# Three edits to the scan stages of a four-layer network: one transfer for B and C, an earlier first map, norm products set apart

## The chip, the cores and the metric

The kernel runs on one core of a Trainium2 chip. The metric is device time in microseconds (us) of one execution, as the median of several runs; lower is better. A profile of one execution was taken besides. Engines are named as in the profile: PE (TensorE, matmuls; PEld its weight loads), DVE (VectorE), ACT (ScalarE), POOL (GpSimd) and SP (SyncE, which here only issues transfers). "Chunk", "step" and "tile" are explained below.

## The reference, cut to what matters

The input is 8 images of 64 channels by 64 x 64 pixels, all in float32, and passes through four layers. Layer 0 is a spectral layer that the change leaves alone. Layers 1, 2 and 3 are built around a selective scan over a sequence with 16 states per channel. Layer 1 scans each image in four ways, layer 2 once, and layer 3 in two stages (along one image axis and then the other), each forward and backward. The core of all of them is this, with layer 3's norm ahead of it:

```python
def rms_norm(x, w):
    return x * lax.rsqrt(jnp.mean(x * x, axis=-1, keepdims=True) + EPS) * w
...
xc = silu(causal_dwconv(xc, cw, cb))          # the "first map" and its convolution
dbl = xc @ xpw.T                              # dt's low-rank part, B and C
dt = jax.nn.softplus(dbl[..., :r] @ dtw.T + dtb)
Bm = dbl[..., r:r + n]
Cm = dbl[..., r + n:r + 2 * n]
A = -jnp.exp(Alog)
...
h = h * dA + (dt_t * x_t)[:, :, None] * B_t[:, None, :]     # dA = exp(dt * A), for each position
y = jnp.einsum('bdn,bn->bd', h, C_t)
...
y = (y + Dp * xc) * silu(z)
```

## The kernel before, in words

**Steps and tiles.** Every scan stage runs through one function, `stream` (L404). Its work is a list of steps. A step is 128 channels by 1024 positions (in layer 3: 256 channels by 512, put side by side). For each of the 16 states n, a step has one tile, 128 x 1024; the text counts tiles by n, and calls the time of one tile a slot. A tile takes these operations:

- SP broadcasts row n of B and of C from HBM to 128 partitions, as `bc`, or as `b` and `c` in layer 1 (L1220, L1602, L1985).
- POOL multiplies B with du = dt * u into `hb` (L465), three tiles ahead in layers 2 and 3, two in layer 1.
- ACT computes `dA` = exp(A * dt) into one of two PSUM buffers (L472), two tiles ahead.
- DVE scans (L481), in place in `dA`, or, for "shared" tiles, into `h`. Shared are tiles 1, 4, 7, 10, 13 of a step; in layer 3's backward steps 2, 6, 10, 14.
- The product with C (L495) is made by DVE, or by POOL for shared tiles.
- PE adds the product to the PSUM tile `acc` with a matmul by the identity (L287), two slots after the scan; a new step begins with a "skip" matmul of u. In layers 1 and 2, ACT copies each scan's last column into `carry` (L1230, L1611) for the step that follows in the same sequence.

When tile 2 of the next step has been scanned, DVE takes the finished `acc` of the last one (the drain: `img` at L1247, `z` at L1620 in layer 2 and L1994 in layer 3).

**What runs beside the tiles.** The order of instructions on each engine is written by hand: `stream` walks the slots, and in each it also lets other generators go on by one piece, up to their next `yield`. The first is `prepare` of the next step, which starts at slot `start`. In layer 2 it loads `x0` with two transfers on SP (L1560), makes the first map `px` on PE (L1567), applies a silu into `u` on ACT (L1570), multiplies u by the weights that give dt's part, B and C (`dbl`, copied out of PSUM by ACT at L1575), sends B and C to HBM in `bc` (L1578; in layer 1 L1203 and L1206), makes `dt` (a softplus, L396), `du` on POOL and the gate `z`. The second is the queue `behind`: in layer 1 the norms and the feed-forward part of other images, in layer 3 `begin` (L1852). A piece that says `CALM` waits for a slot in which neither this tile nor the next is shared; pieces that need the one PSUM buffer `mm` wait for each other; `yield False` lets a slot pass.

**Layer 3's norm.** A chunk is half an image, 8 steps (four groups, each forward and backward). While it is scanned, `begin` prepares the next one: it loads `raw`, squares it, takes means on PE (`ms`), gathers them in `rs`, a square root on ACT (L1879), a reciprocal on DVE (L1881), then sends `rs` to HBM (L1884) and back as a broadcast, `inv` (L1888, two transfers), and POOL multiplies `raw` by `inv` into `xn` in four products of 128 x 560 (L1896), in four slots that follow each other.

**Pools.** Tiles of a name come from a pool with a fixed number of buffers (`dA` 2 in PSUM, `hb` 4, `hc` 4, `bc` 8 in layers 2 and 3); semaphores are put in by the program builder where a buffer is used again. Which buffer a tile gets is also the builder's choice.

Of the kernel before, what the change touches and what calls it, by code (L numbers as in the profile page):

```python
# [10 lines left out]
F32 = mybir.dt.float32  # L11
# [10 lines left out]
NS = 16  # L22
T = 1024
# [226 lines left out]
class Net:  # L250
# [589 lines left out]
    def layer1(self, src, dst):  # L840
        nc, tc, d = self.nc, self.tc, self.d
        mid = self.hbm["x1a"]
        with ExitStack() as ctx:
# [317 lines left out]
            behind = deque()  # L1161
# [21 lines left out]
            class Step:  # L1183
# [12 lines left out]
                def prepare(self):  # L1196
                    k = self.k
                    u = self.u = view(images[self.b]["u"], k, self.c)
                    pd = pp.tile([128, T], F32, name="mm")[:68]
                    net.mm(pd, xp[:, k, :], u)  # L1200
                    yield True
                    dbl = p1.tile([68, T], F32, name="dbl")
                    nc.scalar.copy(dbl, pd)  # L1203
                    self.bc = hp.tile([NS, 2, T], F32, name="bc")
                    for m in range(2):
                        nc.scalar.dma_start(self.bc[:, m, :], dbl[4 + m * NS : 4 + m * NS + NS])  # L1206
                    pt = pp.tile([128, T], F32, name="mm")
                    for r in range(2):
                        at, o = slice(r * C, r * C + 4), slice(r * 512, r * 512 + 512)
                        nc.tensor.matmul(pt[:, o], dtw[at, k, :], dbl[at, o], start=True, stop=True)  # L1210
                    yield True
                    yield CALM
                    dt = self.dt = p2.tile([128, T], F32, name="dt")
                    net.softplus_act(dt, pt, dtb[:, k : k + 1])
                    yield False
                    du = self.du = p2.tile([128, T], F32, name="du")
                    nc.gpsimd.tensor_tensor(like(du, u), like(dt, u), u, ALU.mult)

                def load(self, n, m, t):
                    nc.sync.dma_start(t, self.bc[n : n + 1, m, :].to_broadcast([128, T]))  # L1220

                def first(self, n):
                    if n == 0:
# [274 lines left out]
    def l2_scan(self, hx, hy):  # L1498
        nc, tc, d = self.nc, self.tc, self.d
        with ExitStack() as ctx:  # L1500
# [34 lines left out]
            carries = {}  # L1535

            class Step:
                bc_shape, start, early, late = [128, 2, T], 1, 0, False
                shared = (1, 4, 7, 10, 13)
                rev = False  # L1540
                shaped = staticmethod(lambda t: t)
                spread = staticmethod(lambda t, m: t[:, m, :])
                lanes = [(slice(None), A)]
# [4 lines left out]
                def ready(self):  # L1548
                    pass

                def prepare(self):
                    b, c = self.b, self.c

                    x0 = self.x0 = p2.tile([128, T + 4], F32, name="x0", bufs=3)
                    for r in range(2):
                        lo = c * T - 3 - r
                        if c == 0:
                            nc.gpsimd.memset(x0[r * C : r * C + C, : 3 + r], 0.0)
                        skip_ = max(0, -lo)
                        nc.sync.dma_start(x0[r * C : r * C + C, skip_ : T + 3 + r], hx[b, :, lo + skip_ : c * T + T])  # L1560
                    yield False
                    yield
                    px = pp.tile([128, T], F32, name="mm")
                    for o in (0, 512):
                        for m in range(2):
                            f = o + 3 - 2 * m
                            nc.tensor.matmul(px[:, o : o + 512], taps[:, m, :], x0[:, f : f + 512], start=m == 0, stop=m == 1)  # L1567
                    yield CALM
                    u = self.u = p2.tile([128, T], F32, name="u")
                    nc.scalar.activation(u, px, AF.Silu, bias=cb)  # L1570
                    pd = pp.tile([128, T], F32, name="mm")[:68]
                    net.mm(pd, xp, u)
                    yield True
                    dbl = p1.tile([68, T], F32, name="dbl")
                    nc.scalar.copy(dbl, pd)  # L1575
                    self.bc = hp.tile([NS, 2, T], F32, name="bc")
                    for m in range(2):
                        nc.scalar.dma_start(self.bc[:, m, :], dbl[4 + m * NS : 4 + m * NS + NS])  # L1578
                    pt = pp.tile([128, T], F32, name="mm")
                    for r in range(2):  # L1580
                        at, o = slice(r * C, r * C + 4), slice(r * 512, r * 512 + 512)
                        nc.tensor.matmul(pt[:, o], dtw[at], dbl[at, o], start=True, stop=True)
                    yield CALM
                    dt = self.dt = p2.tile([128, T], F32, name="dt")
                    net.softplus_act(dt, pt, dtb)
                    yield
                    du = self.du = p2.tile([128, T], F32, name="du")
                    nc.gpsimd.tensor_tensor(du, dt, u, ALU.mult)
                    pz = pp.tile([128, T], F32, name="mm")
                    for r in range(2):  # L1590
                        at, f = slice(r * C, r * C + C), 3 + r + r * 512
                        nc.tensor.matmul(
                            pz[:, r * 512 : r * 512 + 512], w_in[at, 128:], x0[at, f : f + 512], start=True, stop=True
                        )
                    yield True
                    yield CALM
                    z = self.z = p2.tile([128, T], F32, name="z", bufs=3)
                    nc.scalar.activation(z, pz, AF.Silu)

                def load(self, n, t):  # L1600
                    row = self.bc[n : n + 1].rearrange("o m t -> o (m t)")
                    nc.sync.dma_start(t.rearrange("p m t -> p (m t)"), row.to_broadcast([128, 2 * T]))  # L1602

                def first(self, n):
                    if n == 0:
# [19 lines left out]
            net = self  # L1625
            with tc.manual_schedule():
                steps = [Step(b, c) for b in range(NB) for c in range(4)]
                self.stream(pools, (6, 3, 6), steps, deque())

    def leaky(self, out, ps):  # L1630
# [157 lines left out]
    def l3_stage(self, s, src, dst):  # L1788
# [6 lines left out]
        with ExitStack() as ctx:  # L1795
# [56 lines left out]
            def begin(c):  # L1852

                b, part = divmod(c, 2)
                q, rows = b // 2, slice((b % 2) * C, (b % 2) * C + C)
                x = raw[c % 2]
                hold = chunks[c] = {"x": x}
                from_ = src[q, rows, part * 4 * W : (part + 1) * 4 * W].rearrange("p (s t) -> p s t", t=HW)
                for r in range(2):
                    nc.sync.dma_start(x[r * C : r * C + C, :, ends[r]], from_)  # L1860
                yield False
                yield False
                rs = p1.tile([128, 16], F32, name="rs")
                for j in range(2):
                    yield CALM_FREE
                    sq = p1.tile([C, T], F32, name="sq")
                    o = sq.rearrange("p (s t) -> p s t", t=HW)
                    nc.scalar.activation(o, x[:C, j * 2 * H : (j + 1) * 2 * H, ends[0]], AF.Square)
                    yield
                    ps = pp.tile([128, T], F32, name="mm")  # L1870
                    self.mm(ps[:1, :], mean, sq)
                    yield CALM
                    ms = p1.tile([1, T], F32, name="ms")
                    nc.scalar.copy(ms, ps[:1, :])
                    yield False
                    nc.sync.dma_start(rs[j * 64 : j * 64 + 64], ms.rearrange("o (p e) -> o p e", e=16))
                yield False
                yield CALM_FREE
                nc.scalar.activation(rs, rs, AF.Sqrt, bias=self.eps5)  # L1879
                yield False  # L1880
                nc.vector.reciprocal(rs, rs)  # L1881
                yield False
                row = hp.tile([1, 4 * W], F32, name="rs")
                nc.sync.dma_start(row.rearrange("o (p e) -> (o p) e", e=16), rs)  # L1884
                yield False
                yield False
                for r in range(2):
                    nc.sync.dma_start(  # L1888
                        inv[r * C : r * C + C, :, ends[r]], row.rearrange("o (s t) -> o s t", t=HW).to_broadcast([C, 4 * H, HW])
                    )  # L1890
                yield False
                yield False
                hold["xn"] = p2.tile([128, 4 * H, HW + 6], F32, name="xn")
                for g in range(4):
                    at = slice(g * H, g * H + H)
                    nc.gpsimd.tensor_tensor(hold["xn"][:, at], x[:, at], inv[:, at], ALU.mult)  # L1896
                    yield False

            behind = deque()
            begun = {}  # L1900
# [162 lines left out]
```

## Time and profile before

| | |
|---|---|
| Median of 3 runs | 25114.63 us (25111.57 to 25133.84) |
| The profiled execution's own time | 25139.42 us |
| Its span | 25137.3 us |
| Busy: DVE, POOL, PE, ACT | 90%, 88%, 85%, 59% of the span |
| Layer 1's scans | about 1245 to 8590 us |
| Layer 2's scans | about 9060 to 10820 us |
| Layer 3's two stages | about 11710 to 25137 us |

Busy time is the time in which an engine executes; the rest is idle, and the profile tells for each instruction how long its engine stood idle before it and what ended that. Two or three engines that are each almost fully busy feed one another through a few buffers, so a wait of one of them can be made good later, or not, depending on how far ahead it was.

### The profile page before, as it was taken

Reading aid. Unit: us, or ns where it says so; the run is one execution under the profiler, and the core shown is the slowest. Engines: PE = TensorE matmul, PEld = TensorE weight load, DVE = VectorE, ACT = ScalarE, POOL = GpSimd, SP = SyncE. Lnnn points to the kernel's source line nnn. Section 1 sums busy time; section 2 is a strip of 40 time slices with the busy share of each in tenths; the row PEclk is TensorE's granted clock in tenths of the full one; section 3 lists DMA queues with packets and bytes.
Section 4 is the critical chain, followed back from the end, with each engine's and each line's share of the span. In section 5 each row is a group of like instructions: output and inputs, shape, how many; then the busy total and the mean of one; then the engine's idle time right before and its main releaser. Section 6 shows DMA issues by size and latency. Waiting matters only on the chain. (4 is left out here: it accounts for less than half of the span.)

```text
span 25137.3 us, 193414 instructions
## 1 busy us (share of the span) xinstructions
PE 21345.1 (85%) x53146; PEld 8321.9 (33%) x53146; DVE 22518.6 (90%) x13020; ACT 14745.8 (59%) x18563; POOL 21997.8 (88%) x10775
## 2 busy tenths in 40 slices
PE   8777888888888888888888888888888888888888
PEld 6522333333333323322333333333333333333333
DVE  5389999989989679978999999999989999999999
ACT  4355555555555455524666666666656666666666
POOL 0099999999989669977999999999989999999999
PEclk9888999999999999999999999999989999999999
DMA  2289898898889658833555545555445554555554
GB/s 64 86 309 320 309 320 313 307 314 314 311 312 314 225 218 323 326 111 87 168 170 168 170 168 171 169 170 168 167 155 171 166 171 165 173 166 172 166 171 158
DMA packets 1772400, 5282.72 MB, mean 210 GB/s; under 512 B 536352, under 2 KB 542564, under 8 KB 1703472
## 3 DMA queue, kind: packets, MB, share of 16 engines
q1 hardware_dynamic: 1744176, 5207.00, 61.0%
q10 hardware_dynamic: 27136, 63.34, 0.8%
q8 instruction: 423, 6.93, 0.1%
q14 instruction: 665, 5.45, 0.1%
HBM read 5112.85 MB, written 156.11 MB: 210 GB/s over the span
## 5 line engine op out<-in xcount | busy, mean ns | idle before, releaser
L465 POOL TENSOR_TENSOR hb<-du,bc 128x1024 f32<-128x1024 f32 x4608 | 10751.5, 2357 | 481.9 <-DVE h L481 330.0
L287 PE MATMUL acc<-hc,ident 128*128 128x512 f32 x18816 | 8899.3, 615 | 93.9 <-DVE img L1247 66.6
L472 ACT ACTIVATE dA<-dt,w_A 128x512 f32<-128x512 f32 x8192 | 5661.7, 691 | 4106.0 <-DVE hc L495 3120.0
L481 DVE TENSOR_TENSOR_SCAN dA<-dA,hb 128x1024 f32<-128x1024 f32 x3384 | 7725.9, 2283 | 285.1 <-ACT dA L472 121.9
L287 PE MATMUL acc<-h,ident 128*128 128x512 f32 x7808 | 4545.1, 712 | 2344.5 <-POOL h L495 2344.1
L287 PEld LDWEIGHTS acc<-hc,ident 128*128 128x128 f32 x18816 | 3695.7, 200 | 5305.9 <-issue 4670.3
L465 POOL TENSOR_TENSOR hb<-du,b 128x1024 f32<-128x1024 f32 x2048 | 4832.7, 2387 | 526.3 <-DVE h L481 279.3
L495 DVE TENSOR_TENSOR hc<-dA,bc 128x1024 f32<-128x1024 f32 x3296 | 4035.6, 1224 | 255.0 <-issue 4.0
L472 ACT ACTIVATE dA<-dt,w_l_A 128x1024 f32<-128x1024 f32 x2560 | 2856.3, 1117 | 1186.5 <-DVE hc L495 757.4
L481 DVE TENSOR_TENSOR_SCAN dA<-dA,carry,hb 128x1024 f32<-128x1024 f32 x1320 | 3094.7, 2344 | 171.2 <-ACT carry L1230 112.3
L287 PEld LDWEIGHTS acc<-h,ident 128*128 128x128 f32 x7808 | 1546.3, 215 | 5004.0 <-POOL h L495 3136.3
L481 DVE TENSOR_TENSOR_SCAN h<-dA,hb 128x1024 f32<-128x1024 f32 x1352 | 3082.5, 2280 | 46.3 <-ACT dA L472 41.4
L495 POOL TENSOR_TENSOR h<-h,bc 128x1024 f32<-128x1024 f32 x1312 | 3090.2, 2355 | 14.5 <-DVE h L481 14.5
L495 DVE TENSOR_TENSOR hc<-dA,c 128x1024 f32<-128x1024 f32 x1408 | 1723.5, 1224 | 114.9 <-DMA c<-bc 4.4
L495 POOL TENSOR_TENSOR h<-h,c 128x1024 f32<-128x1024 f32 x640 | 1516.3, 2369 | 7.4 <-ACT carry L1230 6.5
L481 DVE TENSOR_TENSOR_SCAN h<-dA,carry,hb 128x1024 f32<-128x1024 f32 x600 | 1404.8, 2341 | 80.7 <-ACT dA L472 75.5
L472 ACT ACT_TABLE_LOAD x1122 | 1439.5, 1283 | 21.0 <-ACT tmp L1016 1.2
L1230 ACT COPY carry<-dA 128x1 f32<-128x1 f32 x1056 | 167.9, 159 | 1725.7 <-DVE hc L495 1666.0
L1930 PE MATMUL mm<-xn,taps 128*128 128x512 f32 x2048 | 938.8, 600 | 33.6 <-POOL xn L1896 31.4
L702 POOL MEMSET xf<- 128x24 f32 x33 | 4.3, 142 | 855.8 <-PE ps L723 699.8
L1945 PE MATMUL mm<-u,w_xp 128*36 128x512 f32 x1024 | 519.6, 632 | 146.4 <-ACT u L1942 141.8
L1965 POOL TENSOR_TENSOR du<-dt,u 128x1024 f32<-128x1024 f32 x256 | 602.0, 2352 | 18.9 <-ACT dt L396 18.9
(310 smaller groups left out, 18559.8 us busy)
## 6 DMA issues: line engine op xcount, KB each, us to landing
bc<-bc SPq DMA_DIRECT2D x4096, 512.0 KB
b<-bc SPq DMA_DIRECT2D x2048, 512.0 KB
c<-bc SPq DMA_DIRECT2D x2048, 512.0 KB
bc<-bc SPq DMA_DIRECT2D x512, 1024.0 KB
tmp<-rs SPq DMA_DIRECT2D x93, 512.0 KB
raw<-x SPq DMA_DIRECT2D x64, 512.0 KB
inv<-rs SPq DMA_DIRECT2D x64, 512.0 KB
tmp<-x SPq DMA_DIRECT2D x192, 128.0 KB
```

The source lines that it names most:

```text
L287: self.nc.tensor.matmul(o, lhsT, r, start=start, stop=stop)
L465: nc.gpsimd.tensor_tensor(s.shaped(hb[i]), s.shaped(s.du), B.pop(i), ALU.mult)
L472: nc.scalar.activation(dA[i][:, cut], s.dt[:, cut], AF.Exp, scale=A[:, n : n + 1])
L481: nc.vector.tensor_tensor_scan(h[:, way], dA[i][:, way], hb.pop(i)[:, way], s.first(n), ALU.mult, ALU.add)
L495: engine.tensor_tensor(s.shaped(o), s.shaped(h), CC.pop(i), ALU.mult)
L702: nc.gpsimd.memset(x[:, :, HW:], 0.0)
L1230: nc.scalar.copy(self.carry[:, n : n + 1], h[:, last : last + 1])
L1930: nc.tensor.matmul(tokens(px[:, j * W : j * W + W]), taps[k][:, m, j * 128 : j * 128 + 128], xn[:, :, f : f + HW], start=m == 0, stop=m == 1,)
L1945: nc.tensor.matmul(pd, xp[:, k, j, :], u[:, j * W : j * W + W], start=j == 0, stop=j == 1)
L1965: nc.gpsimd.tensor_tensor(du, dt, u, ALU.mult)
```

## The change

1. In layers 1 and 2, `bc` in HBM becomes 32 rows (16 of B, then 16 of C) in place of 16 rows of pairs, and ACT sends it with one transfer of 32 rows in place of two of 16. Layer 2's broadcast of B and C, still one transfer of 1 MB for each tile, then reads two rows that lie apart; layer 1's reads are as before.
2. In layer 2, a step's `x0` is loaded at the end of `prepare` of the step before (`fetch`, with a fourth buffer), and `prepare` begins with the first map. It starts at slot 2 in place of 1, but has lost two pieces, so that the map stands one slot earlier, ahead of the drain.
3. In layer 3, one more slot passes between the square root and the reciprocal, and nine slots pass after each of the first three products by `inv` in place of one.

```diff
 # layer 1
-                    self.bc = hp.tile([NS, 2, T], F32, name="bc")
-                    for m in range(2):
-                        nc.scalar.dma_start(self.bc[:, m, :], dbl[4 + m * NS : 4 + m * NS + NS])
+                    self.bc = hp.tile([2 * NS, T], F32, name="bc")
+                    nc.scalar.dma_start(self.bc, dbl[4 : 4 + 2 * NS])
...
-                    nc.sync.dma_start(t, self.bc[n : n + 1, m, :].to_broadcast([128, T]))
+                    nc.sync.dma_start(t, self.bc[m * NS + n : m * NS + n + 1, :].to_broadcast([128, T]))
 # layer 2 (its bc is written as in layer 1)
-                bc_shape, start, early, late = [128, 2, T], 1, 0, False
+                bc_shape, start, early, late = [128, 2, T], 2, 0, False
+                behind = None
...
-                def prepare(self):
+                def fetch(self):
                     b, c = self.b, self.c
-                    x0 = self.x0 = p2.tile([128, T + 4], F32, name="x0", bufs=3)
+                    x0 = self.x0 = p2.tile([128, T + 4], F32, name="x0", bufs=4)
...
                         nc.sync.dma_start(x0[r * C : r * C + C, skip_ : T + 3 + r], hx[b, :, lo + skip_ : c * T + T])
-                    yield False
-                    yield
+                def prepare(self):
+                    x0 = self.x0
                     px = pp.tile([128, T], F32, name="mm")
...
                     nc.scalar.activation(z, pz, AF.Silu)
+                    if self.behind:
+                        self.behind.fetch()
                 def load(self, n, t):
-                    row = self.bc[n : n + 1].rearrange("o m t -> o (m t)")
-                    nc.sync.dma_start(t.rearrange("p m t -> p (m t)"), row.to_broadcast([128, 2 * T]))
+                    rows = self.bc.rearrange("(m n) t -> n m t", m=2)[n : n + 1]
+                    nc.sync.dma_start(t, rows.to_broadcast([128, 2, T]))
...
+                for step, other in zip(steps, steps[1:]):
+                    step.behind = other
+                steps[0].fetch()
 # layer 3, begin
                 nc.scalar.activation(rs, rs, AF.Sqrt, bias=self.eps5)
                 yield False
+                yield False
                 nc.vector.reciprocal(rs, rs)
...
                     nc.gpsimd.tensor_tensor(hold["xn"][:, at], x[:, at], inv[:, at], ALU.mult)
-                    yield False
+                    for _ in range(9 if g < 3 else 1):
+                        yield False
```

More of the change, by code (lines that the diff above doesn't have):

```diff
@@ L1575, in prepare @@
                     nc.scalar.copy(dbl, pd)
-                    self.bc = hp.tile([NS, 2, T], F32, name="bc")
-                    for m in range(2):
-                        nc.scalar.dma_start(self.bc[:, m, :], dbl[4 + m * NS : 4 + m * NS + NS])
+                    self.bc = hp.tile([2 * NS, T], F32, name="bc")
+                    nc.scalar.dma_start(self.bc, dbl[4 : 4 + 2 * NS])
                     pt = pp.tile([128, T], F32, name="mm")
```

## The prediction

> **What bounds the kernel now.** I read the page first (busy time, then the costliest groups), then the busy times by stage, then each scan's waits, then the order in time around those waits.
>
> ```profile
> PE 21345.1 (85%) x53146; PEld 8321.9 (33%) x53146; DVE 22518.6 (90%) x13020; ACT 14745.8 (59%) x18563; POOL 21997.8 (88%) x10775
> ...
> L465 POOL TENSOR_TENSOR hb<-du,bc 128x1024 f32<-128x1024 f32 x4608 | 10751.5, 2357 | 481.9 <-DVE h L481 330.0
> ```
>
> DVE and POOL both carry the span. By stage (columns: length, then busy time and count of PE, PEld, DVE, ACT and POOL, clock, DMA share, GB/s) these are layer 1's scans, layer 2's, and layer 3's second half:
>
> ```profile
> 1245.00:8590.00 7345.00, 6196.51 (x13857) 2333.71 (x13858) 6658.71 (x3717) 3900.18 (x4865) 6736.96 (x2960) 0.92 0.89 313
> 9060.00:10820.00 1760.00, 1423.96 (x3054) 542.66 (x3056) 1618.54 (x896) 1026.12 (x1241) 1632.98 (x718) 0.90 0.84 322
> 18460.00:25137.00 6677.00, 5744.65 (x11990) 2180.78 (x11989) 6445.34 (x3661) 4434.87 (x5768) 6456.22 (x2935) 0.94 0.52 168
> ```
>
> Neither engine can be shortened here, only DVE's waits can go: 686 us in layer 1, 142 in layer 2, some 520 in layer 3. The view of waits names them; the first three lines are layer 3's, the next three layer 2's.
>
> ```profile
> DVE z L1994 <- PE acc L287: 157.7, 41, 5.6
> DVE rs L1881 <- ACT rs L1879: 49.6, 31, 16.9
> DVE dA L481 <- POOL hb L465: 8.1, 10, 1.8
> ...
> DVE h L481 <- ACT dA L472: 59.7, 28, 4.6
> DVE dA L481 <- ACT carry L1611: 26.5, 20, 2.3
> ...
> ACT L1570 <- PE mm L1567: 87.6, 30, 3.4
> ```
>
> **Part 1, one transfer (layers 1 and 2).** It removes 160 DMA issues from ACT (two took 0.78 us in layer 1, 0.90 in layer 2). An issue in itself is worth little, since ACT then mostly waits for DVE. The order of instructions with their semaphores shows more. In layer 1 the dA that follows the pair of issues (tile 5) often waits not for tile 3's readers but for tile 4's scan, since the pool gave it tile 4's PSUM buffer. One such step in the order in time (ACT, then DVE):
>
> ```profile
> 1842.72 1.12 ACT L472 ACTIVATE dA<-dt,w_l_A 128x1024 f32<-128x1024 f32 x1 [2.10 <-DVE h L481]
> ...
> 1843.94 2.36 DVE L481 TENSOR_TENSOR_SCAN dA<-dA,carry,hb 128x1024 f32<-128x1024 f32 x1 [1.25 <-ACT carry L1230]
> ```
>
> ACT was free 2.10 us earlier; DVE loses the 1.25 us in which dA is made. Counted in the two orders, 88 of layer 1's steps have this wait in the old kernel and 43 in the new one; layer 2 keeps its 24. So 45 x 1.25 = 56 us; POOL idles 1 to 2 us in most such steps, so it follows nearly all the way. I take **-54** (bounds -30, if POOL binds, and -56). Other steps of layer 1 keep their waits.
>
> The same edit makes layer 2's loads read two rows of 4 KB where they read one of 8 KB: 256 packets for 128. In the trace's DMA packets a packet of 8192 bytes takes 334 ns on average in layer 2; of 4096 bytes, 185 in layer 1's loads. A load on 16 engines is then 16 x 185 = 2.96 us for 8 x 334 = 2.67, plus 0.22 a tile of other packets (111 us of 16 engines over 512 tiles): 3.18 against the 3.27 us a tile that I forecast for layer 2. POOL waited for loads 6 times, 5.9 us in all, and loads run six tiles ahead, so I cost it at 0; without that cover it is the third rival.
>
> **Part 2, layer 2's first map.** Its px matmuls move on PE from behind the drain, the skip and tile 1's gather to ahead of them; PE stood 4.3 us there waiting for the drain (9515.54), so they cost PE nothing. ACT's order does not change. ACT's silu waited for px 30 times, 2.9 us each; now it starts 2.65 us earlier (9523.52 for 9526.17), and the scan of tile 7, which lost 1.9 to 2.5 us to it, finds its dA. Next late is dA of tile 8: in 24 steps it shares tile 7's buffer and can't start before that scan ends, so 24 x 1.25 = 30 us stay. Layer 2's DVE waits, 104.9 us in the view (the above and 11.5, 7.2), less 5 at the start and these 30, leave 70. POOL, 51.0 us busy a step, has room below the 52 that DVE then needs. The x0 transfers (two issues of 0.59 us on SP) go out a step earlier, into a fourth buffer: 0. I take **-62** (-20 to -70; the low end if the buffers between POOL and DVE turn half of it into other waits).
>
> **Part 3, layer 3.** 30 of the 32 chunks run beside scans. Their step (drain to drain) lasts 57.1 us on average, the same step without products 50.64. The excess, 6.5: z 4.74, reciprocal 1.09, hb 0.26, the reciprocal itself 0.2, small ones. Here are two products, then the drain:
>
> ```profile
> 12325.25 1.37 POOL L1896 TENSOR_TENSOR xn<-raw,inv 128x560 f32<-128x560 f32 x1 [1.93 <-DMA inv<-rs]
> ...
> 12328.88 1.37 POOL L1896 TENSOR_TENSOR xn<-raw,inv 128x560 f32<-128x560 f32 x1
> ...
> 12354.56 1.22 DVE L1994 TENSOR_TENSOR z<-acc,z 128x1024 f32<-128x1024 f32 x1 [4.37 <-PE acc L287]
> ```
>
> *The reciprocal* moves behind one more scan and product, 3.5 us, so its 1.09 us wait goes: 33 us. But ACT's chain there (silu, sqrt, three table loads) ends dA at 12304.76, and a DVE no longer held up asks for it at 12304.5: 0.3 comes back. Net -24. The transfers behind it (SP: one row, two inv) move one tile with it, and so does the first product; POOL waited for inv 0.4 us a chunk, and I leave that.
>
> *The products*: 4 x 1.37 = 5.5 us of POOL in four tiles delay the h products, hence PE's last gather and the drain. In the new order they stand before h(10), after h(13), after h(6) of the next pair and after h(14). POOL regains 0.64 + 0.69 + 1.16 = 2.5 us a pair in its waits for DVE, so the first and the third each reach h(14) as a lag of 1.37. Two lines of PE tell what that does, without products and with:
>
> ```profile
> 12135.72 1.98 PE L287 MATMUL acc<-h,ident 128*128 128x512 f32 x4 [2.73 <-POOL h L495]
> ...
> 12764.47 3.78 PE L287 MATMUL acc<-h,ident 128*128 128x512 f32 x4 [4.37 <-POOL h L495]
> ```
>
> PE's wait becomes 2.73 + 1.37 = 4.10. All 14 waits of 4.0 to 4.5 us in layer 3 (the shortest 4.19) were followed by slow matmuls (1.06 us and more a record); at 3.0 to 3.5 most stayed at 0.6. Slow, acc is ready 6.15 us after h(14)'s end (12764.4 to 12770.6); fast, 3.54. DVE arrives 6.42 after it when POOL is on time. So the drain waits 1.37 - 0.27 = 1.1 us, twice a chunk. The second and fourth stand behind their step's last h; the drain they can delay has 1.6 to 3.3 us to spare against a lag of 1.0: 0.1. Hence 2.3 for 4.74 + 0.26: -81. Together **-105** (bounds -50, if lags add up, and -177, if PE stays fast).
>
> [...] The 14 of 14 rows speak for slow each time.
>
> **Sum.** 54 + 62 + 105 = 221. Against the profiled execution (25139.4, span 25137.3) that is 24,918; it lies 24.8 above the runs' median, so I give **24,895**.
>
> **Rivals.**
> - *The products vanish altogether*: if at 4.10 us PE stays fast, 3.54 + 1.37 is below 6.42 and no drain waits: 69 us more, 24,825. For it: the wait of 3.91 began fast. Against it: all from 4.19 up are slow.
> - *Waits change places*: POOL, at 51 us a step beside DVE's 52, becomes the bound in layers 1 and 2, and lags add up in layer 3: 30 + 20 + 50 = 100, so 25,015. For it: POOL shows only 0.1 us idle in one of layer 1's steps. Against it: layer 3's ordinary steps run without any DVE wait at the same load.
> - *Layer 2's loads become the bound* (slower): if 4 KB packets there take what layer 2's other 4 KB packets take, 245 ns, a load is 3.92 + 0.22 = 4.14 us a tile for 3.44 now: 512 x 0.70 = +358 in place of -62, so 25,115 + 358 - 54 - 105 = 25,314. It decides from 191 ns a packet on (16 x 191 + 220 = 3.27), and the whole is slower than before from 220 or so. Against it: layer 1 at 185 and a DMA share of 0.89 hardly waits. That margin is thin.
> - *The edit does not do what it says*: not here; the order shows each move.
>
> **Chances.** Forecast 0.62, first rival 0.17, second 0.12, third 0.05, something unseen 0.04. The range reaches from the first rival to past the second, widened by the bounds: 24,810 to 25,040. About 0.2%, 50 us, is what a measurement of this kernel can tell from no change: faster 0.90, same 0.05, slower 0.05.
>
> **What would show it.** Layer 2 (9060 to 10820) some 60 us shorter, with ACT's wait for px gone and tile 8's 1.25 left in 24 steps; layer 1 with 45 fewer 1.25s; in layer 3 no rs wait, z waits halved and near 1.1 each, at twice as many places. Wrong: long POOL waits for bc in layer 2, or z waits of 4 us.

## The result, and the profile after

| | before | after |
|---|---|---|
| Median | 25118.15 us (25111.57 to 25133.84, 4 runs) | 24936.65 us (24932.17 to 24940.46, 4 runs) |
| Profiled execution, its span | 25139.42, 25137.3 | 24935.87, 24934.1 |
| Layer 1, first scan to last | 7336.1 | 7293.2 (-43.0) |
| Layer 2 | 1746.6 | 1678.1 (-68.5) |
| Layer 3, two stages | 6659.5 + 6668.4 | 6622.3 + 6612.7 (-93.0) |

The ratio is 0.9925, interval 0.9913 to 0.9936: 182 us faster by the medians, 203 by the two profiled spans. Between the stages nothing moved by more than 2.7 us. Stage lengths, here and below, are from the start of the stage's first scan to the end of its last.

The page of the changed kernel, its busy times and the group that answers to the one shown of before:

```profile
PE 21183.9 (85%) x53146; PEld 8266.9 (33%) x53146; DVE 22534.6 (90%) x13020; ACT 14735.8 (59%) x18563; POOL 22026.2 (88%) x10775
...
L465 POOL TENSOR_TENSOR hb<-du,bc 128x1024 f32<-128x1024 f32 x4608 | 10740.3, 2356 | 294.6 <-DVE h L481 186.5
```

DVE's and POOL's work is what it was (22534.6 for 22518.6, 22026.2 for 21997.8); only idle time went. POOL's idle time ahead of these products fell from 481.9 to 294.6 us. By stage (the columns as before: length, busy times with counts, clock, DMA share, GB/s), layer 1, layer 2, and layer 3's second half:

```profile
1245.00:8547.00 7302.00, 6171.31 (x13860) 2327.64 (x13860) 6656.41 (x3717) 3899.89 (x4865) 6778.05 (x2960) 0.92 0.90 315
9021.00:10713.00 1692.00, 1403.56 (x3051) 524.64 (x3050) 1615.75 (x896) 1021.13 (x1239) 1631.30 (x718) 0.93 0.96 334
18312.00:24934.10 6622.10, 5680.84 (x11991) 2163.27 (x11989) 6449.07 (x3661) 4432.22 (x5768) 6448.86 (x2934) 0.95 0.51 169
```

Layer 2's DMA share rose from 0.84 to 0.96 with the shorter steps and the two rows a load. Its waits of DVE (time, times, longest), where before had 59.7, 26.5 and 11.5 us in three lines of dA and carry:

```profile
DVE dA L481 <- ACT carry L1613: 36.8, 30, 3.5
DVE dA L481 <- POOL hb L465: 25.3, 1, 25.3
DVE z L1622 <- PE acc L287: 2.1, 1, 2.1
DVE dA L481 <- ACT dA L472: 1.9, 3, 1.3
```

The 25.3 is the stage's first tile. What ACT's silu waited for is gone, as its line in time shows: the table load and the silu follow each other with no idle time in brackets.

```profile
9466.43 1.28 ACT L1571 ACT_TABLE_LOAD   x1
9467.73 1.11 ACT L1571 ACTIVATE u<-mm,w_l_cb 128x1024 f32<-128x1024 f32 x1
```

Layer 3's waits of DVE, first scan to last:

```profile
DVE dA L481 <- ACT dA L472: 76.4, 34, 33.8
DVE z L2002 <- PE acc L287: 51.2, 68, 3.9
DVE h L481 <- ACT dA L472: 42.1, 53, 0.8
DVE rs L1887 <- ACT rs L1884: 16.8, 1, 16.8
```

The drain (z) waits 51.2 us where it waited 154.9; the reciprocal's wait is down to one at the start of a stage; and a wait that before hardly had (5.2 us) has come, h for dA, 42.1 us. POOL got one too. The view of POOL's waits in layer 3's scans, before and then after:

```profile
POOL xn L1896 <- DMA inv<-rs: 50.8, 12, 39.7
```

```profile
POOL xn L1902 <- DMA inv<-rs: 93.5, 31, 39.2
```

Without the one long wait at a stage's start, that is 11.1 us in 11 chunks before, and 54.3 in 30 after: nearly every chunk, 1.8 us each.

### The profile page after: what moved, and what is told of

The parts are those of the page before. It is cut to its first block, busy times and chain, and to the rows that moved or that the text cites. A ratio compares the mean times of both kernels' runs of the same rounds, so it can differ in the third digit from the quotient of the medians.

```text
span 24934.1 us, 193361 instructions
## 1 busy us (share of the span) xinstructions
PE 21183.9 (85%) x53146; PEld 8266.9 (33%) x53146; DVE 22534.6 (90%) x13020; ACT 14735.8 (59%) x18563; POOL 22026.2 (88%) x10775
## 5 line engine op out<-in xcount | busy, mean ns | idle before, releaser
L465 POOL TENSOR_TENSOR hb<-du,bc 128x1024 f32<-128x1024 f32 x4608 | 10740.3, 2356 | 294.6 <-DVE h L481 186.5
L495 DVE TENSOR_TENSOR hc<-dA,c 128x1024 f32<-128x1024 f32 x1408 | 1723.0, 1224 | 132.5 <-DMA c<-bc 22.4
```

Of the source, the lines that this page charges most:

```text
L465: nc.gpsimd.tensor_tensor(s.shaped(hb[i]), s.shaped(s.du), B.pop(i), ALU.mult)
L495: engine.tensor_tensor(s.shaped(o), s.shaped(h), CC.pop(i), ALU.mult)
```

## The experiments

The theory after the result: (1) layer 1 gains by the dA buffers, layer 2 by the earlier map, as predicted; (2) in layer 3 the spacing gives more than the whole, and the reciprocal's slot costs, because it makes `inv` late. The rivals: layer 1 gains by the issue it saves; the slot costs nothing, or costs by where it puts the products. Stage lengths of unchanged code differ by up to 17 us from trace to trace (layer 1 took 7284 to 7301 us in the six kernels that have the change's code for it; layer 3 has the same code in three of the kernels below: -131, -118, -129).

### Layer 1

**l1_merge**: before, with the one transfer of B and C in layer 1 alone.

```diff
-                    for m in range(2):
-                        nc.scalar.dma_start(self.bc[:, m, :], dbl[4 + m * NS : 4 + m * NS + NS])
+                    nc.scalar.dma_start(self.bc, dbl[4 : 4 + 2 * NS])
...
```

> The kernel before with one transfer for B and C in layer 1 alone. Theory (the buffer): the order of instructions has the same 45 fewer tiles whose dA gets the PSUM buffer of the tile before it, so layer 1 (first scan to last, 7336 us before, 7293 in the changed kernel) is 43 us shorter, the rest unchanged: about -43 us. Rival (the issue): ACT has one transfer fewer to issue in each of 128 steps, 0.33 us each, 42 us at most: about the same here; the next kernel tells the two apart. Rival (another stage helped layer 1): less than half of 43.

Measured: 25089.07 for 25134.1 us, ratio 0.9983 (0.9974 to 0.9993); layer 1 took 7295.5, 40.6 less.

**l1_alternate**: before, both transfers kept; in layer 1 the dA tiles take the two PSUM buffers in turn, by name.

```diff
-                dA[i] = pe.tile([128, T], F32, name="dA")
+                dA[i] = pe.tile([128, T], F32, name=f"dA{i % 2}" if self.alternate else "dA")
...
```

> The kernel before, with both transfers kept, but in layer 1 tile i's dA has buffer i modulo 2 by name, so that none of the 160 repeated buffers is left. Theory (the buffer): layer 1 gains more than the 43 us of the 45, since 130 of its waits of DVE for ACT were about 1.25 us: -80 to -150 us, less where POOL becomes the bound. Rival (the issue): two issues a step are still there, so 0, within 10 us.

Measured: 25086.42 us, ratio 0.9982 (0.9973 to 0.9991); layer 1 took 7291.0, 45.2 less. So the buffers alone can give the gain, with both issues left in. That they are its cause in l1_merge shows in which steps got shorter. Steps are timed here from the scan of tile 3 to that of the next step's tile 3, in the mean of six traces with the change's layer 1 against five with the old one. The 46 steps in which tile 5's dA no longer starts after tile 4's scan are 0.67 us shorter each, 31 of 44 us in all. The other 81 are 0.16 us shorter each, which is the most that the saved issue can be worth; and the 38 of them that never had this wait gain as much (0.19 us each) in l1_alternate, where both issues stay. But l1_alternate's size was far off its forecast. In the order in time, the scans that waited for a dA which itself had waited for DVE's scan lost 151.3 us in 120 places before, 101.6 in 81 with l1_merge, 96.6 in 77 in the changed kernel, and none here. Where the rest of the 151 went is in the waits of DVE in layer 1, before and then l1_alternate:

```profile
DVE dA L481 <- ACT carry L1230: 170.7, 130, 3.1
DVE dA L481 <- POOL hb L465: 77.7, 20, 65.1
...
DVE dA L481 <- ACT dA L472: 65.7, 51, 2.8
```

```profile
DVE dA L486 <- ACT dA L477: 114.5, 86, 3.7
DVE dA L486 <- POOL hb L470: 106.3, 62, 64.9
DVE tmp L1118 <- PE mm L911: 70.8, 28, 6.2
```

The first line of before is all but gone (9.5 us left). Waits for a dA that ACT makes late, behind other work of its own, rose by 49, for POOL's hb by 29 in three times as many places (62 for 20), for a matmul of the feed-forward part by 15. A wait taken away in layer 1 uncovers the next engine's lateness behind it.

### Layer 2

**l2_map**: before, with the second part of the change alone (`fetch`, the first map one slot earlier).

```diff
-                bc_shape, start, early, late = [128, 2, T], 1, 0, False
+                bc_shape, start, early, late = [128, 2, T], 2, 0, False
...
-                    yield False
-                    yield
...
```

> The kernel before with layer 2's earlier first map (and x0 a step ahead) alone: two transfers to HBM and rows of 8 KB as before. Theory: the whole of layer 2's gain is here: first scan to last 1678 us or a little less, for 1746.6, so about -68 us. Rival (the merge paid part of it, by its shorter ACT queue at tile 8): -40 or less.

Measured: 25060.35 us, ratio 0.9971 (0.9961 to 0.9981); layer 2 took 1675.4, 71.2 less.

**l2_merge**: before, with layer 2's one transfer and its loads of two rows of 4 KB, the map where it was.

```diff
...
-                    row = self.bc[n : n + 1].rearrange("o m t -> o (m t)")
+                    rows = self.bc.rearrange("(m n) t -> n m t", m=2)[n : n + 1]
...
```

> The kernel before with layer 2's one transfer and its loads of two rows of 4 KB alone. Theory: the loads stay hidden and the issue was not on the path except at tile 8, whose dA in 24 steps waits for tile 7's scan anyway: 0, within 10 us. Rival (packets): twice the packets cost time in a stage whose DMA share is 0.84 already: layer 2 longer by 10 us or more. Rival (issue): 0.45 us less on ACT in each of 32 steps, up to -14.

Measured: 25128.74 us, ratio 1.0000 (0.9990 to 1.0009); layer 2 took 1741.6, 5 less. POOL's waits for these loads rose, but no engine passed them on. The view of its waits in layer 2, l2_merge:

```profile
POOL hb L465 <- DMA bc<-bc: 32.6, 25, 5.6
```

The 4 KB packets took 182 ns on average in this layer 2, and 184 in the changed kernel's. So layer 2's whole gain is the map's, and the smaller packets cost nothing that can be measured, here or in the changed kernel (22.6 us of such waits on POOL, while DVE waited for hb once, at the start).

### Layer 3

**l3_spread**: before, with the nine slots between the products and no added slot.

```diff
-                    yield False
+                    for _ in range(9 if g < 3 else 1):
+                        yield False
```

> The kernel before with layer 3's products nine slots apart, but no slot added ahead of the reciprocal. Theory (the inv transfers): the reciprocal's wait of 1.09 us stays (33 us), but the inv transfers stay ahead of the load that waits for POOL's h product, so POOL waits for inv in about a third of the chunks and not in all 30 (11 us, not 54), lags are 1.4 us smaller and the z and dA waits that the changed kernel has in layer 3 (54 and 51 us) are well below half. Layer 3: about -90 to -120 us, as much as or more than the -93 of both edits together. Rival (the slot pays by itself): the edits add up, so this alone gives -93 + 24 = -70 or less.

Measured: 25001.12 for 25124.05 us, ratio 0.9950 (0.9936 to 0.9965); layer 3 took 131 less. Its drain hardly waits any more (waits of DVE in layer 3):

```profile
DVE rs L1881 <- ACT rs L1879: 66.4, 32, 17.1
DVE z L1996 <- PE acc L287: 23.9, 35, 2.8
DVE h L481 <- ACT dA L472: 21.3, 27, 0.8
```

**l3_recip**: before, with the added slot alone.

```diff
                 yield False
+                yield False
                 nc.vector.reciprocal(rs, rs)
```

> The kernel before with the slot ahead of the reciprocal alone; the four products still follow each other. Theory (the inv transfers): the reciprocal's wait goes (-33 us), but POOL waits for inv about 1.8 us in each of 30 chunks, so the drain's wait grows by about as much (+40): 0 to +20 us in all. Rival (prediction's step): -24 us.

Measured: 25152.78 us, ratio 1.0012 (1.0002 to 1.0021): slower by 29, layer 3 by 27. The reciprocal's waits are gone, and yet (waits of DVE, then of POOL, in layer 3):

```profile
DVE z L1995 <- PE acc L287: 187.1, 42, 6.8
```

```profile
POOL xn L1897 <- DMA inv<-rs: 138.4, 32, 40.4
```

The drain waits 32 us more than before's 154.9. Of POOL's line two waits (80 us) are the starts of the stages; the other 30 sum to 58.4. Why inv is late stands in SP's order in time: rs goes to HBM (first of the lines, L1884 or L1890), then loads of bc, then inv (L1888, L1894). A row with x2 reaches from the first issue's start to the second's end. Before, and then the changed kernel:

```profile
12307.16 0.38 SPq L1884 DMA_DIRECT2D rs<-rs  x1
12307.63 1.96 SPq L1985 DMA_DIRECT2D bc<-bc  x2
12311.50 5.20 SPq L1888 DMA_DIRECT2D inv<-rs  x2
12316.79 11.28 SPq L1985 DMA_DIRECT2D bc<-bc  x5
```

```profile
13019.99 0.38 SPq L1890 DMA_DIRECT2D rs<-rs  x1
13020.90 7.26 SPq L1993 DMA_DIRECT2D bc<-bc  x2
13028.26 3.68 SPq L1894 DMA_DIRECT2D inv<-rs  x2
```

One slot later, inv stands on SP behind a load of bc whose buffer is not free yet: from rs to inv it takes 8.27 us in place of 4.34 (in the median 8.3 in place of 4.0). In all 30 chunks prepared beside scans the profile puts the wait of one of the two loads between rs and inv down to POOL's h product, in the changed kernel as in l3_recip; in before, l3_spread, inv_back and inv_only it does so in none.

**inv_back**: the changed kernel, with the slot between the reciprocal and rs's transfer taken out, so that rs, inv and the products go one slot earlier.

```diff
                 nc.vector.reciprocal(rs, rs)
-                yield False
                 row = hp.tile([1, 4 * W], F32, name="rs")
```

> The changed kernel, with the transfer of rs to HBM issued in the piece of the reciprocal, one slot earlier, so that it and the two inv transfers stand where they stood before the change, ahead of the load that waits for POOL's h product. Theory (the inv transfers): POOL's wait for inv, 54 us in 30 chunks, nearly goes; layer 3's z and dA waits (54 and 51 us) halve: -40 to -60 us against the changed kernel, -220 to -240 against the kernel before. Rival (the lag comes from the products alone): POOL's wait goes, but the time stays within 10 us of the changed kernel.

Measured: 24907.08 us, ratio 0.9913 (0.9898 to 0.9927). Layer 3 took 23 less than in the changed kernel, and the waits for inv fell from 54.3 to 29.2, in 25 chunks: half of the cause, half of the effect, since the products come a slot earlier too. Its four runs lie 40 us apart, so the size is rough.

**no_recip**: the changed kernel without the added slot.

```diff
                 nc.scalar.activation(rs, rs, AF.Sqrt, bias=self.eps5)
                 yield False
-                yield False
```

> The changed kernel without the added slot before layer 3's reciprocal. The traces of the runs before give, for layer 3's two stages together, 93 us less than before with the slot and spacing, and 131 less with the spacing alone. If that difference is the slot's own cost: 38 us less than the changed kernel, some 24,898 us (ratio to before 0.9912). If the three parts share a gain that a faster layer 3 can't have twice, the same as the changed kernel.

Measured: 24889.61 for 25117.15 us, ratio 0.9910 (0.9895 to 0.9925); layer 3 took 25 less than in the changed kernel. The slot as it stands is a loss.

By then there were two readings of why. The steps of a chunk differ (mean length in us from one drain to the next; step 2 holds all four products before, and the first of them in the others; the mean is over all 32 chunks, and the last of each stage has no products beside it):

| step | before | l3_recip | l3_spread | after | fourth_back | inv_only |
|---|---|---|---|---|---|---|
| 2 | 56.73 | 57.43 | 51.98 | 51.71 | 51.66 | 51.34 |
| 3 | 51.83 | 51.82 | 52.22 | 52.05 | 52.11 | 51.82 |
| 4 | 50.69 | 50.81 | 51.43 | 51.38 | 51.47 | 51.16 |
| 5 | 52.00 | 51.91 | 51.80 | 52.51 | 52.51 | 51.96 |
| 6 | 50.39 | 50.40 | 50.36 | 51.18 | 51.22 | 51.02 |

After is no longer than l3_spread where inv is waited for (step 2), but it is at steps 5 and 6, behind the last product, which the slot moves on by one tile. So the place of the products could be the cause as well as inv. The next two kernels tell these apart.

**fourth_back**: the changed kernel, with the fourth product one tile earlier, where l3_spread has it.

```diff
-                    for _ in range(9 if g < 3 else 1):
+                    for _ in range((9, 9, 8, 1)[g]):
```

> The changed kernel with eight slots in place of nine after the third product, so that the fourth stands one tile earlier, where the spacing without the slot has it; the slot and the waits for inv stay. Theory A, the slot costs by the place of the fourth product (in the changed kernel the steps five and six drains into a chunk are 0.7 and 0.8 us longer than with the spacing alone): 30 x 1.5 = 45 us less than the changed kernel. Theory B, it costs by the waits for inv (54 us of POOL): no change, within 10 us.

**inv_only**: the changed kernel, with rs and inv sent one slot earlier and all four products left in place.

```diff
                 nc.vector.reciprocal(rs, rs)
-                yield False
                 row = hp.tile([1, 4 * W], F32, name="rs")
...
                 yield False
                 yield False
+                yield False
                 hold["xn"] = p2.tile([128, 4 * H, HW + 6], F32, name="xn")
```

> The changed kernel with the two transfers of inv (and rs's ahead of them) one slot earlier, and all four products where the changed kernel has them. Theory B, the waits for inv cost: POOL's waits for inv go from 54 us to near 10, and the kernel is 20 to 45 us faster. Theory A, the place of the fourth product costs: the waits for inv shrink, and the time stays within 10 us, since the steps five and six drains into a chunk keep their z and dA waits.

Measured: fourth_back 24924.29 us (24913.18 to 24940.69), ratio 0.9924 (0.9912 to 0.9937), layer 3 4 us longer than in the changed kernel; inv_only 24883.85 (24870.01 to 24886.85), ratio 0.9906 (0.9893 to 0.9920), layer 3 54 less. In inv_only POOL no longer waits, and the drain waits 19 us (waits of POOL, then of DVE, in layer 3):

```profile
POOL xn L1902 <- DMA inv<-rs: 40.2, 3, 39.5
```

```profile
DVE h L481 <- ACT dA L472: 29.7, 38, 0.8
DVE z L2002 <- PE acc L287: 19.1, 38, 2.8
```

So inv it is: 54 us of waits on POOL were worth 54 us of layer 3 in the traces (53 by the medians of inv_only and the changed kernel, 40 by those of inv_only and fourth_back). The table shows how a 1.8 us wait in step 2 is paid: 0.4 at once, 0.2 in each of the next two steps and the largest share, 0.55, at step 5 (52.51, then 51.96), presumably since POOL, as busy as DVE here, works off its lag slowly. The fourth product's place is worth nothing at step 5. What stays longer in inv_only is step 6; it is 51.0 to 51.2 in the three kernels with the later products and 50.36 in l3_spread, no_recip and inv_back, so it goes with the places of the first three products; which of them was not tried.

### Versions that beat both

**best** is inv_back with dA buffers in turn in layers 1 and 2 (the line shown under l1_alternate), **best2** is no_recip with the same.

> The changed kernel with the rs transfer one slot earlier, and in layers 1 and 2 tile i's dA in buffer i modulo 2. Theory (the buffer): layer 2 loses its 24 waits of 1.25 us (-30, if POOL at 51 us a step lets it), layer 1 another -40 to -100 beside the 43 that it had; with the inv transfers back in their place -300 to -400 us against the kernel before. Rival (the issue): layers 1 and 2 as in the changed kernel, so about -230.

> The changed kernel without the added slot, and with layers 1 and 2 taking their dA buffers in turn by name. The turn-taking was worth some 36 us in the run that had it with inv sent a slot earlier (15 in layer 1, 23 in layer 2), the slot's removal some 15 us more than that sending: 24,857 us, ratio to before 0.9895; the fastest version of the study, if the gains add up. If not, 24,872 or more.

Measured: best 24871.97 us, ratio 0.9899 (0.9883 to 0.9916); best2 24865.47 (24847.01 to 24871.64), ratio 0.9899 (0.9885 to 0.9912). Layer 2 took 1656 and 1663 us for the changed kernel's 1678; layer 1 7286 and 7275 for 7284 to 7301 in the six kernels with the change's layer 1. Both are faster than the changed kernel; of the gain that best expected from the turns most failed to come in layer 1, probably for the reason that l1_alternate shows (in best's layer 1 DVE waits 93.0 us for hb and 88.2 for a dA that ACT makes late, for 84.7 and 59.4 in the changed kernel). Turns and inv_only together were not tried.

## Why the prediction came out nearly right

**The sum.** 221 us were forecast from one profiled execution to the next, 203 came. The median forecast was 42 us too low: 18 of them are the sum's, and 24 came because the 24.8 us by which before's profiled execution lay above its median were taken off as if they belonged to the kernel; after's lay 0.8 below its own.

**Layer 1: -54 forecast, -43 measured.** The mechanism holds: 43 waits of the named kind went (45 forecast), 39 of them at tile 5, 54.7 us in all. The step that failed is "it follows nearly all the way", and not for the bound given there (POOL): DVE's waits for C's loads rose from 4.4 to 22.4 us, for the feed-forward's matmuls by 8.5 and for hb by 7. (Other lines moved by up to 7 us either way.) The waits for C came with the single transfer: 17 to 25 us in six traces that have it, 30 and 37 in best and best2, mostly at tiles 8, 12 and 15, and 4 to 5 us in the six that don't, l1_alternate among them, where layer 1 is as short. The forecast priced that edit's data side at nothing in layer 1. Why those tiles' loads are late, whether by where C's rows now lie or by the order of the transfers, stays open.

**Layer 2: -62 forecast, -68.5 measured.** All steps came as stated: the map ahead of the drain, px no longer waited for, tile 8's waits left (24 x 1.25 = 30 us forecast; 31.4 in 23 places, of the 36.8 in the line above; the rest is at tile 0), and no cost of the 4 KB packets at a DMA share of 0.96. The third rival is ruled out by l2_merge, and by the packets' 182 to 184 ns, near the 185 of the forecast and far from that rival's 245.

**Layer 3: -105 forecast, -93 measured, by two errors that nearly cancel.** That the sum came near is luck here.

*The products* were mis-sized: -81 forecast, -131 in l3_spread (-126 in the mean of the three kernels with layer 3's spacing alone). The step that failed is "PE's wait becomes 2.73 + 1.37 = 4.10", and with it "slow" and the 1.1 us at the drain. PE in the changed kernel, around a first product that had also waited 1.40 us for inv (PE's lines in time, idle time in brackets):

```profile
12205.49 5.42 PE L287 MATMUL acc<-hc,ident 128*128 128x512 f32 x12
12218.45 3.78 PE L287 MATMUL acc<-h,ident 128*128 128x512 f32 x4 [7.55 <-POOL h L495]
12222.02 5.39 PE L287 MATMUL acc<-hc,ident 128*128 128x512 f32 x12
12230.00 1.98 PE L287 MATMUL acc<-h,ident 128*128 128x512 f32 x4 [2.58 <-POOL h L495]
```

The lag shows in the wait before h(10), some 4.8 us without a product (4.77 at 12423.2 of the same trace) and here 7.55 = 4.77 + 1.37 + 1.40. The matmuls that follow h(10) are late by as much, so that the wait before h(14) keeps its length, 2.58, and its four matmuls take 1.98 us. A lag that an engine has already passed on doesn't lengthen its later waits; the prediction counted it a second time. That brings most of the first rival's end (the products vanish, -150) by another way than it gave: no wait near 4.10 had to stay fast. In l3_spread the drains of steps 2 to 4 wait 0.1, 0.3 and 0.0 us, against a forecast of 1.1 twice a chunk. The changed kernel's 51.2 us in 68 places look like that forecast, but most of them are inv's: with inv on time 19.1 us are left.

*The reciprocal* was right by itself and wrong in what followed. Its 33 us of waits went, 8 came back at dA, and with inv on time the slot is worth some 20 us in layer 3 (inv_only's -147 against that -126; -24 was forecast). That is one trace against three that differ by 13; by the medians inv_only is only 6 us faster than no_recip, so the gain itself is not shown. But "The transfers behind it ... move one tile with it ... POOL waited for inv 0.4 us a chunk, and I leave that" is where the gain was lost: the tile that inv moved to has an SP queue held up by a buffer, 1.8 us a chunk, 54 us in all. In short: -126 for the products, some -20 for the slot, +54 for inv's new place. These add up to the -93 measured by the way in which they were taken, as differences between the same stage lengths, so the sum proves nothing by itself; what shows inv's part is inv_only.

*What else came.* The new waits of h for dA (42.1 us) were not forecast. They stand at steps 4 and 6 (of the table), and begin with ACT's copy of dbl. Those of step 4, 19.4 us, come with the spacing (20.9 in l3_spread). Those of step 6, 22.8 us, come with the later places of the products (18.5 in inv_only, under 1 in l3_spread, no_recip and inv_back); they are nearly all of what step 6 is longer by. In the changed kernel, ACT's order in time, then DVE's:

```profile
13123.30 0.58 ACT L1956 COPY dbl<-mm 36x512 f32<-36x512 f32 x1 [2.99 <-PE mm L1953]
13123.78 2.74 ACT L472 ACTIVATE dA<-dt,w_A 128x512 f32<-128x512 f32 x4
```

```profile
13125.29 2.29 DVE L481 TENSOR_TENSOR_SCAN h<-dA,hb 128x1024 f32<-128x1024 f32 x1 [0.81 <-ACT dA L472]
```

The copy waits 2.99 us for a matmul that PE made late, and the dA queued behind it on ACT comes 0.81 us late for DVE.

**The rivals.** Of the second (waits change places), the part "lags add up" was real: inv's lag and the products' added up at step 5. POOL did not become the bound in layers 1 and 2: DVE's waits for hb rose by 7 us in layer 1, and in layer 2 there is only the one at the start. The order of instructions did show every move, as said; it also shows inv's new place on SP behind that load, and there the prediction did not look.

## What to carry to other kernels

When a step moves by one slot, follow its last transfer to the place that it takes in its queue, and ask what the entry ahead of it waits for: one slot later can be four microseconds later (here 8.27 us from rs to inv for 4.34). Price a lag once, at the first wait where it appears; work behind it on the same engine is late by the same amount and its own waits don't grow (here 2.58 us before h(14), for 2.72 in the same trace without a product). In a kernel with two full engines a removed wait is worth what the next late engine leaves of it (here 43 us of 54.7 in layer 1), so measure each part alone and together before adding.

## What the runs showed of the hardware

*The clock after a wait.* In layer 3, over ten of the kernels, 1,374 gathers (matmuls that add a product to `acc`) began after PE had waited 4.0 us or more. 1,370 of them (286 of 287 in before and after) began with slow matmuls (over 0.9 us a record in the mean of the first four, for 0.59 to 0.70), the other four, after 4.17 to 4.19 us, with 0.81 to 0.90. After 3.4 to 3.6 us it was 231 of 424 (42 of 60 in after). The wait that repeats most, of 4.6 to 4.8 us, was followed by slow matmuls every time (154 times in before and after).

The granted clock in the traces of before and after goes with this. It was either 1.0 or 0.5; the records of the gathers in layer 3 took 592 ns in the median at 1.0 and 1061 at 0.5. Its changes lay on a grid of 3.41333 us, within 0.01 us over the whole execution. In layer 3 of the two, all 470 intervals of this grid that were at 1.0 and in which PE was busy for less than 40% were followed by one at 0.5; with PE busy for 40 to 45% it was 75 of 119, and for 45% or more 16 of 6,386. Of the intervals at 0.5, all 262 with PE busy for less than 80% were followed by another at 0.5. By these rows a wait of 2 x 0.6 x 3.41 = 4.1 us (an estimate) leaves some interval at least 60% idle wherever it falls, and one of 3.5 us only in some positions, which fits the counts above.

*Packets.* Two rows of 4 KB for one of 8 KB raised the DMA share of layer 2 from 0.84 to 0.91 at the same speed (l2_merge: 1741.6 us for 1746.6, 322 GB/s in both), and at a share of 0.97, in best2, layer 2 ran 1663 us at 339 GB/s, with DVE waiting for hb only once, at the stage's start. A packet of 8 KB took 334 ns on average in layer 2 before, one of 4 KB 184 in the changed kernel.
